# A fused graph-attention and graph-convolution kernel: the four attention units moved together ahead of the convolution, one fold for all, and w2 sums issued sooner

## The chip, the cores and the metric

The kernel runs on one core of a Trainium2 chip (trn2). The metric is the time of one execution in device microseconds; the median of three runs is given. All data is float32. The core has TensorE (PE in the profile, its weight loads PEld), VectorE (DVE), ScalarE (ACT), GpSimd (POOL) and SyncE (SP), whose queue here issues nearly all DMA transfers.

## The reference

There are 16 batches of x, each 1024 nodes by 256 channels, one dense adjacency matrix of 1024 x 1024, and two layers, each followed by a layer norm. The first is attention whose query comes from a graph product; the second is two graph convolutions.

```python
# layer 0, per batch; x: (N=1024, C=256), 4 heads of 64
c_adj = mean over channels of x                      # (N,)
A     = 2 * | |sigmoid(c_j - c_i) - 0.5| - 0.5 |     # (N, N), then made symmetric
g     = relu((x^T @ (adj * A)) * para)               # (C, N)
q     = g^T split in heads;  k, v = x @ kv_w split in heads
att   = softmax(q k^T * scale) v
x     = layernorm(x + att)
# layer 1
h = relu(x @ w1_loop + adj @ (x @ w1_neigh) + b1)    # (N, 128)
h = relu(h @ w2_loop + adj @ (h @ w2_neigh) + b2)    # (N, 256)
x = layernorm(x + (x + h) * 0.5)
```

## The kernel before

**The stages.** The program is one straight list, written out by hand (`tc.manual_schedule()`): each engine runs its instructions in the order in which `run()` (L1196) emits them, and semaphores between engines follow from the tiles that instructions share. There is no planner. An instruction that waits holds up all behind it on its engine; that goes for SyncE's queue of DMA issues too. Tiles of 128 x 1024 come out of a pool of 31 "row" buffers, PSUM tiles out of three "big" ones (128 x 1024) and two "banks" (128 x 512).

In the loop over batches, batch b's attention is computed beside work for three other batches: query, keys and values of batch b+1, the first convolution of batch b−1 (`c1`), the second of batch b−2 (`c2`), and the normalization and output of batch b−3 (`c3`, which exists from b=3 on). Batches 0, 1 and 15 have branches of their own; batches 2 to 14 share one (L1328 to L1372), which the change rewrites. After the loop an epilogue does the convolutions that are left.

**Attention.** A batch has four units: two pairs of heads, times two halves of 512 query nodes. For each unit `scores` (L688 to L715) multiplies keys and queries (L702, two matmuls of 64 rows each per block of 128 keys, eight blocks) and ScalarE takes the exponential (L707, L709). The eight exponentials are added up by VectorE in `collect` (L721, L723); `partial` turns the sum in blocks of 32 x 32 (L728) and reduces it (L731) to a part of the softmax denominator. `outputs` multiplies exponentials and values (L744); `turn` (L750) transposes the result o in blocks of 32. `add` (L757 to L779) sums the parts over partitions with a small matmul against a constant `fold` (L764), takes reciprocals (L770), multiplies o (L774), adds it to the residual in `xB` (L776), and reduces rows for the layer norm (L777). It is called twice in a batch of this branch: for units 0 and 1 inside the convolution (at `turn_to(2)`), for 2 and 3 inside step 1 of the query.

**The query.** The product x^T @ (adj * A) is done with seven block products in place of eight (class `FastQueries`, Strassen's scheme in a form with fewer additions). `left` (L604 to L609) makes sums S of blocks of x on GpSimd. `likeness` (L560, L561) makes the factor A of a row of blocks on ScalarE, `times_adj` (L566) multiplies it with adj on VectorE, and `right` (L619 to L622) makes sums T of weighted blocks. `step(k)` (L647) is then the matmuls for one of four k, seven products of each. Rows 0 and 4 are weighed in `weigh_first`, 1 and 5 in `weigh_second`, 2 and 6, 3 and 7 in `pair`. `KeysValues` makes keys and values in the same way; `kv.sums()` makes its four K sums on VectorE (L423 to L431), and `kv.load()` (L436) fetches weight sums made once at the start.

**The convolution.** `c1.inner()` (L857) multiplies x by w1_neigh. Then `Joined` (L1103) shares the adjacency product of c1's first and c2's second convolution: both need adj times something with 128 columns, and again seven products are made. Its `left` (L1125 to L1128) makes sums R on GpSimd, `product(n)` (L1134) is four matmuls of 512 columns, and `run` (L1137 to L1177) sets the order: products 1, 2, 6, 7, 5, 4, then product 3 in two halves with c2's last products around it. Between products, ScalarE and VectorE move results out of PSUM (L1153, L1156, L1162, L1166, L1169) and form u's halves (L1173 on VectorE, L1174 on GpSimd). `run` takes a table `between`: for each of some places (`turn_to(1)`, `turn_to(2)` and so on) a list of functions that emit other work there. `block_sums` (L953 to L962) forms sums s1 (L958, GpSimd), s2, s4 and s3 (L960 to L962, VectorE) of c2's data, and `last_products` (L979 to L1002) makes seven products with w2's blocks (L971), collecting them by L984 to L1000 and `settle` (L975). A PSUM bank's next product has to wait until the copy or addition before has read it: product 3 of `last_products` goes to the bank that L993 (`u3 + c`) has read. w2's sums and the step of the bias are fetched in `load_sums` (L947 to L950), and `bias` (L1142) copies rows of them to PSUM; the first use is in `run` after `turn_to(2)`.

**Around it.** `c3.statistics()` (L310, L311) takes mean and variance of c3's rows; `deviation` (L315 on VectorE, L316, a power of −0.5, on GpSimd) makes the reciprocal deviation. `finish_aside` (L1020 to L1027) scales the rows on ScalarE and issues the output transfer. `c1.turn_blocks()` transposes c1's result and writes it to DRAM (h1d, L889), from where `load_h1` (L894) takes it at the start of the next batch, with nodes along the partitions. `NodeSums` (L277 to L300) sums x over channels on ScalarE for c_adj.

In batches 2 to 14 before the change, the order on TensorE is: scores of units 0 and 1, their outputs, `inner`, `Joined.run`, scores of units 2 and 3, their outputs, the four steps of the query, keys and values. `channel_major` (the turned x, xT) and the K sums come with the outputs of units 0 and 1.

Of the kernel before, what the change touches and what calls it, by code (L numbers as in the profile page):

```python
# [18 lines left out]
def kernel(  # L19
# [31 lines left out]
    nc = tc.nc  # L51
# [47 lines left out]
    def row_tile(name):  # L99
        return work.tile([P, N], F32, tag="row", name=name, bufs=ROWS)  # L100
# [483 lines left out]
    class FastQueries(Queries):  # L584
# [16 lines left out]
        def block(self, i, j):  # L601
            return self.xb[:, j * TJ:(j + 1) * TJ, ts(i, P)]

        def left(self, eng):  # L604
            s12, s34 = (row_tile(f"S_{self.b}_{k}").rearrange("p (s t c) -> p s t c", s=2, c=P) for k in range(2))
            eng.tensor_add(s12[:, 0], self.block(1, 0), self.block(1, 1))
            eng.tensor_sub(s12[:, 1], s12[:, 0], self.block(0, 0))
            eng.tensor_sub(s34[:, 0], self.block(0, 0), self.block(1, 0))
            eng.tensor_sub(s34[:, 1], self.block(0, 1), s12[:, 1])  # L609
            self.S = [s12[:, 0], s12[:, 1], s34[:, 0], s34[:, 1]]  # L610
# [63 lines left out]
    class Attention:  # L674
# [5 lines left out]

        def __init__(self, b, xB, qT, kT, v):
            self.b, self.xB, self.qT, self.kT, self.v = b, xB, qT, kT, v
            self.parts, self.o, self.pr = {}, {}, {}

            self.rden = small.tile([P, len(UNITS) * FB // S], F32, tag="rden", name=f"rden_{b}", bufs=2)
            self.sums = small.tile([P, NC, NB], F32, tag="sums", name=f"sums_{b}", bufs=2)
# [38 lines left out]
        def partial(self, u):  # L725
            b = self.b
            accB = row_tile(f"accB_{b}_{u}")
            nc.vector.transpose(accB, self.acc)  # L728
            if u % 2 == 0:
                self.part = small.tile([P, 2, N // S], F32, tag="den_part", name=f"den_part_{b}_{u}", bufs=2)  # L730
            nc.vector.tensor_reduce(self.part[:, u % 2, :], by_node(accB), AX.X, ALU.add)  # L731
            self.parts[u] = self.part

        def both_scores(self, pair, summed=True):
            for j in range(NJ):
# [15 lines left out]
        def turn(self, u):  # L751
# [2 lines left out]
            self.o[u] = work.tile([P, FB], F32, tag="o", name=name) if late else row_tile(name)[:, 0:FB]  # L754
            nc.vector.transpose(self.o[u], pav)

        def add(self, *units):  # L757

            b, half = self.b, FB // S
            u0, n = units[0], len(units)  # L760
            pd = bank_psum(f"den_ps_{b}_{u0}")
            den = pd[:, 0:2 * half * n]
            part = [self.parts.pop(u) for u in units][0]
            nc.tensor.matmul(den, fold.rearrange("p a k -> p (a k)"),  # L764
                             part[:, u0 % 2:u0 % 2 + n, :].rearrange("p u k -> p (u k)"), start=True, stop=True)
            den = den.rearrange("p (u s h) -> p u s h", u=n, s=2)
            rden = self.rden[:, u0 * half:(u0 + n) * half].rearrange("p (u h) -> p u h", u=n)
            for s in range(2):
                rows = slice(s * HD, (s + 1) * HD)
                nc.vector.reciprocal(rden[rows], den[rows, :, s, :])  # L770
            for k, u in enumerate(units):
                pair, j = UNITS[u]
                o = by_node(self.o.pop(u))
                nc.vector.tensor_mul(o, o, rden[:, k, :].unsqueeze(2).to_broadcast([P, half, S]))  # L774
                dst = by_node(self.xB[pair][:, ts(j, FB)])
                nc.vector.tensor_add(dst, dst, o)  # L776
                nc.vector.tensor_reduce(self.sums[:, pair, ts(j, half)], dst, AX.X, ALU.add)  # L777
            if u == len(UNITS) - 1:
                join(self.sums)  # L779
# [62 lines left out]
    class GraphConv:  # L842


        def __init__(self, b, xT, nodes=None, x=None):
            self.b, self.xT, self.nodes, self.x = b, xT, nodes, x

        def load_x(self):
            self.x = xpool.tile([P, NT, C], F32, tag="x", name=f"x1_{self.b}")
# [253 lines left out]
    class Joined:  # L1103
# [33 lines left out]
        def run(self, between=None, last=None):  # L1137
# [19 lines left out]
            turn_to(2)  # L1157
            if last:
                bias(third, b2_sb[:, ts(0, P)])
                c2.load_sums()  # L1160
            self.product(6, first, again=True)
            nc.scalar.copy(u1, first)  # L1162
            c1.relu(0, p1)
# [32 lines left out]
    def run():  # L1196
# [58 lines left out]
        for b in range(B):  # L1255
# [18 lines left out]
                q.times_adj(TJ)  # L1274
                q.right(0)

            def two_units(pair, before_first=lambda: None, before_second=lambda: None):
                u = NJ * pair
                att.outputs(u, half_psum, turned=False)
                before_first()  # L1280
                att.turn(u)
                att.outputs(u + 1, turned=False)
                before_second()
                att.turn(u + 1)

            if more and not c1:
                att.both_scores(0)
                NodeSums(q, xb, str(b + 1)).all()
                two_units(0)
                att.both_scores(1)  # L1290
                for t in range(3):
                    q.load(t)
                    q.weigh(t)
                two_units(1)
            elif more and not both:
                att.scores(0)
                att.outputs(0)
                NodeSums(q, xb, str(b + 1)).all()
                kv = KeysValues(b + 1, channel_major(blocked, f"xT_{b + 1}"))
                att.scores(1)  # L1300
                kv.sums()
                att.add(0)
                att.outputs(1)
                for t in (0, TJ):
                    q.load(t)
                c1.inner()
                q.left(nc.gpsimd)
                for t in (0, TJ):
                    q.likeness(t)
                for ij, n in QUARTERS.items():  # L1310
                    store(n, quarters[ij])
                c1.first(quarters, lambda: (att.add(1), adj_sums(quarters, 1), adj_sums(quarters, 2), weigh_first()))
                c1.turn_blocks()
                att.scores(2)
                att.outputs(2)
                for t in (1, TJ + 1):
                    q.load(t)
                    q.likeness(t)
                    q.times_adj(t)
                att.scores(3)  # L1320
                for t in (2, TJ + 2, 3, TJ + 3):
                    q.load(t)
                for t in (2, TJ + 2, 3, TJ + 3):
                    q.likeness(t)
                q.right(1)
                att.add(2)
                att.outputs(3)
            elif more:  # L1328
                att.both_scores(0, summed=False)
                nodes = NodeSums(q, xb, str(b + 1))  # L1330
                att.collect(1, 1, 2, 3)
                nodes.turn()
                att.collect(1, *range(4, NT))
                att.partial(1)
                both.fetch("00", "10")
                c2.load_x()

                def next_xT():
                    ready["xT"] = channel_major(blocked, f"xT_{b + 1}")

                two_units(0, before_second=next_xT)
                if c3:
                    c3.statistics()
                kv = KeysValues(b + 1, ready["xT"])
                kv.sums()
                both.fetch(2, 3)
                nodes.line()
                both.fetch(1)
                nodes.row()
                for t in (0, TJ):  # L1350
                    q.load(t)
                both.fetch(4, "11")
                c1.inner()
                both.left(nc.gpsimd)
                q.left(nc.gpsimd)
                both.run({1: (lambda: q.likeness(0),),
                          2: (lambda: att.add(0, 1), lambda: q.likeness(TJ), lambda: c3 and c3.deviation(), weigh_first)},
                         last=nc.gpsimd)
                c1.turn_blocks()
                att.both_scores(1)  # L1360
                order = (1, TJ + 1, 2, TJ + 2, 3, TJ + 3)
                for t in order:
                    q.load(t)
                for t in order:
                    q.likeness(t)

                def weigh_second():
                    q.times_adj(1)
                    q.times_adj(TJ + 1)
                    q.right(1)  # L1370

                two_units(1, before_second=weigh_second)  # L1372
            else:
                att.both_scores(0)
                two_units(0)
                att.both_scores(1)
                two_units(1, before_second=lambda: att.add(0, 1))
# [38 lines left out]
            elif more:  # L1416
                q.pair(2)
                q.step(0)
                if c3:
                    c3.finish_aside(out[b - 3])  # L1420
                q.step(1, lambda: att.add(*((2, 3) if both else (3,))), 5)
                q.pair(3)
                q.step(2, norm.mean)
                q.load_para()
# [21 lines left out]
            convs[b] = GraphConv(b, norm.x1T, norm.nodes)  # L1446
        c1, c2, c3, c4 = (convs[B - k] for k in (1, 2, 3, 4))
        both = Joined(c1, c2)
        both.fetch("00", "10", 2, 3, 1, 4, "11")
        quarters = fetch_quarters("e", both.far)  # L1450
        c2.load_x()
        c1.inner()
# [79 lines left out]
```

## Time and profile before

| what | value |
|---|---|
| median of 3 runs | 2136.1 us (2135.74 to 2136.44) |
| profiled execution, own time | 2135.35 us |
| its span | 2133.6 us |
| mean granted TensorE clock | 0.997 |
| busy: PE, PEld | 2116.3 us, 1037.2 us |
| busy: DVE, ACT, POOL | 1907.5 us, 1140.1 us, 359.0 us |
| DMA | 346.39 MB, mean 162 GB/s |
| batch 8 by stages (us from the span's start) | scores and outputs of units 0, 1: 1044.85 to 1072.66; convolution: to 1110.53; units 2, 3: to 1138.34; query, keys and values: to 1175.59 |

A page of the profile gives busy times by engine, a row of 40 slices of the span, the DMA queues, the chain of work that ended last, and the costliest groups of instructions. The trace behind it can be asked for a timeline (start and length in us, engine, line, operation, output and inputs, shapes, number of instructions joined, and in brackets how long the engine was idle before it and what released it) and for a table of waits (engine, line and tile that waited, what it waited for, us in total, how many, longest). PE busy includes matmuls that overlap; their ends are modelled, so differences of starts are the better measure.

### The profile page before, as it was taken

The numbers are of one execution on the slowest core, as the hardware profiler recorded it, in microseconds if no ns is written. First come the engines' busy times: TensorE is split into PE (matmuls) and PEld (weight loads), VectorE is DVE, ScalarE is ACT, GpSimd is POOL, SyncE is SP. The second block draws the span as 40 slices with busy tenths as digits, with TensorE's granted clock in tenths as the row PEclk, the third lists the DMA queues.
The fourth block names the chain that finished last, engine by engine and source line by source line (L and its number), as shares of the span: only waits on it lengthen the run. The fifth ranks groups of instructions, "written<-read, shape, count | busy, mean of one in ns | idle before, by whom it ended". The sixth has DMA issues, their size and how long they took to land.

```text
span 2133.6 us, 25172 instructions
## 1 busy us (share of the span) xinstructions
PE 2116.3 (99%) x8734; PEld 1037.2 (49%) x8734; DVE 1907.5 (89%) x2381; ACT 1140.1 (53%) x1669; POOL 359.0 (17%) x209
## 2 busy tenths in 40 slices
PE   9999999999999999999999999999999999999997
PEld 5344444545545455444454444544454444545454
DVE  7899999989999898998989989899898999989874
ACT  5745545556365563655635555454655546556322
POOL 2010120221303113031130301313012130221111
PEclk9999999999999999999999999999999999999998
DMA  9495666637549284592946829377293763925453
GB/s 222 120 170 193 135 221 146 186 107 141 203 125 272 74 165 169 137 262 70 201 141 150 241 69 233 109 163 228 75 259 103 153 212 106 268 87 107 165 192 112
DMA packets 613718, 346.39 MB, mean 162 GB/s; under 512 B 491984, under 2 KB 556880, under 8 KB 613584
## 3 DMA queue, kind: packets, MB, share of 16 engines
q1 hardware_dynamic: 613312, 344.45, 61.2%
q8 instruction: 71, 1.16, 0.2%
q14 instruction: 63, 0.52, 0.1%
q10 hardware_dynamic: 272, 0.26, 0.0%
HBM read 294.45 MB, written 50.20 MB: 162 GB/s over the span
## 4 chain that ended last, share of the span: by engine, by line
PE 98%; DMA 1%; DVE 1%; ACT 0%; POOL 0%; issue 0%; POOLq 0%; SPq 0%; ACTq 0%; DVEq 0%
PE s L702 21%; PE av L744 21%; PE g_ps L647 16%; PE hu_ps L1134 16%; PE v_ps L448 5%; PE k_ps L444 5%; PE hu_ps L971 4%; PE t_ps L857 3%; PE g_ps L574 3%; PE hu_ps L864 2%; PE h_ps L879 1%; PE u_ps L908 1%; DMA out_dram<-x 1%; PE h_ps L971 1%; DMA w_sums<-w_sums 0%; PE den_ps L764 0%
## 5 line engine op out<-in xcount | busy, mean ns | idle before, releaser
L723 DVE TENSOR_TENSOR acc<-acc,pr 128x1024 f32<-128x1024 f32 x384 | 472.2, 1230 | 37.4 <-DVE acc L723 1.4
L702 PE MATMUL s<-qT,kT 64*128 64x512 f32 x2048 | 449.7, 593 | 0.0
L744 PE MATMUL av<-pr,v 128*64 128x512 f32 x2048 | 447.0, 594 | 0.0
L709 ACT ACTIVATE pr<-s 128x1024 f32<-128x1024 f32 x392 | 390.7, 1115 | 75.6 <-PE s L702 75.6
L702 PEld LDWEIGHTS s<-qT,kT 64*128 64x128 f32 x2048 | 196.3, 187 | 232.7 <-issue 183.3
L744 PEld LDWEIGHTS av<-pr,v 128*64 128x64 f32 x2048 | 144.0, 137 | 297.4 <-issue 272.6
L361 POOL TENSOR_TENSOR rstd<-rstd,neg_half 128x32 f32<-128x32 f32 x16 | 99.3, 6203 | 1113.2 <-DVE rstd L359 1113.2
L1134 PE MATMUL hu_ps<-adj,R 128*128 128x512 f32 x480 | 214.3, 594 | 0.0
L560 ACT ACTIVATE wg<-c_row,c_sums 128x1024 f32<-128x1024 f32 x120 | 137.0, 1142 | 81.4 <-DVE den_part L731 60.3
L566 DVE SCALAR_TENSOR_TENSOR wg<-wg,adj 128x1024 f32<-128x1024 f32 x128 | 150.0, 1211 | 3.6 <-ACT wg L561 3.6
L707 ACT ACTIVATE pr<-s 128x512 f32<-128x512 f32 x240 | 142.4, 702 | 0.3 <-PE s L702 0.3
L1134 PEld LDWEIGHTS hu_ps<-adj,R 128*128 128x128 f32 x480 | 89.0, 190 | 100.9 <-issue 99.5
L561 ACT ACTIVATE wg<-wg 128x1024 f32<-128x1024 f32 x128 | 135.3, 1057 | 4.1
L860 ACT COPY t<-t_ps 128x1024 f32<-128x1024 f32 x16 | 16.2, 1012 | 189.6 <-PE t_ps L857 189.6
L647 PE MATMUL g_ps<-wg,S 128*128 128x512 f32 x224 | 115.5, 597 | 0.0
L647 PE MATMUL g_ps<-T,S 128*128 128x512 f32 x224 | 115.5, 597 | 0.0
L647 PE MATMUL g_ps<-wg,x 128*128 128x512 f32 x224 | 109.0, 599 | 0.0
L1134 PE MATMUL hu_ps<-adj,t 128*128 128x512 f32 x240 | 105.7, 592 | 0.0
L1125 POOL TENSOR_TENSOR R<-h 128x512 f32<-128x512 f32 x14 | 28.2, 2012 | 359.5 <-PE av L744 238.8
L721 DVE TENSOR_TENSOR acc<-pr,pr 128x1024 f32<-128x1024 f32 x64 | 77.5, 1211 | 12.3 <-ACT pr L709 12.3
L728 DVE STREAM_TRANSPOSE accB<-acc 128x1024 f32<-128x1024 f32 x64 | 79.7, 1245 | 2.2
L731 DVE TENSOR_REDUCE den_part<-accB 128x32 f32<-128x1024 f32 x64 | 78.1, 1220 | 2.2
(235 smaller groups left out, 3120.1 us busy)
## 6 DMA issues: line engine op xcount, KB each, us to landing
adj<-adjT SPq DMA_DIRECT2D x210, 512.0 KB
adj<-in_adj_dram SPq DMA_DIRECT2D x128, 512.0 KB
para<-in_L_gnn_para_dram SPq DMA_DIRECT2D x32, 512.0 KB
xB_a<-in_x_dram SPq DMA_DIRECT2D x128, 128.0 KB
x1d<-xB_a SPq DMA_DIRECT2D x128, 128.0 KB
x<-x1d SPq DMA_DIRECT2D x16, 1024.0 KB
xB<-in_x_dram SPq DMA_DIRECT2D x120, 128.0 KB
x<-in_x_dram SPq DMA_DIRECT2D x15, 1024.0 KB
```

What stands on the lines that cost most here:

```text
L444: nc.tensor.matmul(dst, self.a[0][n], self.w[n], start=not again, stop=True, skip_group_check=again)
L448: nc.tensor.matmul(dst[:, ts(t, P)], self.w[n][:, ts(t, P)], self.a[1][n], start=not again and t == 0, stop=True, skip_group_check=again o ...
L560: nc.scalar.activation(wg, self.c_row, AF.Abs, bias=self.c_col[:, t:t + 1], scale=-1.0)
L561: nc.scalar.activation(wg, wg, AF.Tanh, scale=-0.5 / C)
L566: nc.vector.scalar_tensor_tensor(wg, wg, 1.0, self.adj.pop(t), op0=ALU.add, op1=ALU.mult)
L647: nc.tensor.matmul(self.p[n], x_n[:, k, :], w_n, start=(k == 0), stop=(k == TJ - 1))
L702: nc.tensor.matmul(halves[s], self.kT[rows, pair, ts(mt, P)], self.qT[rows, pair, ts(j, FB)], start=True, stop=True)
L707: nc.scalar.activation(pr[:, ts(s, FB)], halves[s], AF.Exp)
L709: nc.scalar.activation(pr, ps, AF.Exp)
L723: nc.vector.tensor_add(self.acc, self.acc, prs[mt])
L744: nc.tensor.matmul(pav[s * HD:(s + 1) * HD, :], self.v[:, mt, pair * P + s * HD:pair * P + (s + 1) * HD], prs[mt][:, ts(s, FB)], start=(mt ...
L1134: nc.tensor.matmul(dst, self.x[n][:, k, :], of_rows(rows, k), start=(start and k == 0), stop=(k == TJ - 1), skip_group_check=again)
```

## The change

Four things change. (1) In batches 2 to 14 all four attention units come first, with both of a pair's o tiles in one row (`both_outputs`), and the convolution follows; after it the query's steps come directly. (2) The denominators of all four units stand in one tile, and `add_all` folds them with one matmul of 128 columns, takes reciprocals over all, and multiplies, adds and reduces 1024 columns at a time. It stands at `turn_to(2)` of the convolution, and the two calls of `add` go. (3) Much that stood between the two halves of attention moves: `channel_major` and S come after `inner`, S into the buffers of the blocked x that has been turned (`rows`); S is made before R; K sums and the second `times_adj` move to `turn_to(4)`, behind s1 to s4 on VectorE; the rest of the weighing's likenesses and `finish_aside` move to `turn_to(3)`, that is to the convolution's end, ahead of `turn_blocks`; `weigh_first` moves from `turn_to(2)` to `turn_to(1)`. (4) In the epilogue, `load_sums` is called ahead of `c2.load_x()` and not in `run`.

```diff
-        def left(self, eng):
-            s12, s34 = (row_tile(f"S_{self.b}_{k}").rearrange("p (s t c) -> p s t c", s=2, c=P) for k in range(2))
+        def left(self, eng, rows=None):
+            rows = rows or [row_tile(f"S_{self.b}_{k}") for k in range(2)]
+            s12, s34 = (row.rearrange("p (s t c) -> p s t c", s=2, c=P) for row in rows)
...
+        def both_outputs(self, pair, between=lambda: None):
+            u = NJ * pair
+            row = row_tile(f"o_{self.b}_{pair}")
+
+            def turn(u, j):
+                pav, self.o[u] = self.o[u], row[:, ts(j, FB)]
+                nc.vector.transpose(self.o[u], pav)
+
+            self.outputs(u, turned=False)
+            self.collect(u + 1, 1, 2, 3)
+            between()
+            self.collect(u + 1, 4, 5)
+            turn(u, 0)
+            self.collect(u + 1, 6, 7)
+            self.partial(u + 1)
+            self.outputs(u + 1, half_psum, turned=False)
+            turn(u + 1, 1)
+            self.o[u] = row
+
+        def add_all(self):
+            b, half, n = self.b, FB // S, len(UNITS)
+            pd = bank_psum(f"den_ps_{b}")
+            nc.tensor.matmul(pd[:, 0:n * NB], fold.rearrange("p a k -> p (a k)"),
+                             self.part.rearrange("p u k -> p (u k)"), start=True, stop=True)
+            den = pd[:, 0:n * NB].rearrange("p (u s h) -> p u s h", u=n, s=2)
+            rden = self.rden.rearrange("p (u h) -> p u h", u=n)
+            for s in range(2):
+                rows = slice(s * HD, (s + 1) * HD)
+                nc.vector.reciprocal(rden[rows], den[rows, :, s, :])
+            for pair in range(NC):
+                o = by_node(self.o.pop(NJ * pair))
+                nc.vector.tensor_mul(o, o, self.rden[:, ts(pair, NB)].unsqueeze(2).to_broadcast([P, NB, S]))
+                dst = by_node(self.xB[pair])
+                nc.vector.tensor_add(dst, dst, o)
+                nc.vector.tensor_reduce(self.sums[:, pair, :], dst, AX.X, ALU.add)
+            join(self.sums)
...
             if last:
                 bias(third, b2_sb[:, ts(0, P)])
-                c2.load_sums()
+                if c2.w2 is None:
+                    c2.load_sums()
...
             elif more:
-                att.both_scores(0, summed=False)
+                att.scores(0, 0)
+                att.scores(1, NT, summed=False)
                 nodes = NodeSums(q, xb, str(b + 1))
-                att.collect(1, 1, 2, 3)
-                nodes.turn()
-                att.collect(1, *range(4, NT))
-                att.partial(1)
+                c2.load_x()
+                att.both_outputs(0, nodes.turn)
+                nodes.line()
+                nodes.row()
+                att.scores(2, 0)
+                att.scores(3, NT, summed=False)
                 both.fetch("00", "10")
-                c2.load_x()
-
-                def next_xT():
-                    ready["xT"] = channel_major(blocked, f"xT_{b + 1}")
-
-                two_units(0, before_second=next_xT)
+                for t in (0, TJ):
+                    q.load(t)
+                    q.likeness(t)
+                both.fetch(2, 3)
+                att.both_outputs(1)
+                c1.inner()
+                xT_next = channel_major(blocked, f"xT_{b + 1}")
+                q.left(nc.gpsimd, blocked)
+                both.left(nc.gpsimd)
                 if c3:
                     c3.statistics()
-                kv = KeysValues(b + 1, ready["xT"])
-                kv.sums()
-                both.fetch(2, 3)
-                nodes.line()
+                kv = KeysValues(b + 1, xT_next)
                 both.fetch(1)
-                nodes.row()
-                for t in (0, TJ):
+                for t in (1, TJ + 1):
                     q.load(t)
                 both.fetch(4, "11")
-                c1.inner()
-                both.left(nc.gpsimd)
-                q.left(nc.gpsimd)
-                both.run({1: (lambda: q.likeness(0),),
-                          2: (lambda: att.add(0, 1), lambda: q.likeness(TJ), lambda: c3 and c3.deviation(), weigh_first)},
+
+                def more_weights():
+                    for t in (2, TJ + 2, 3, TJ + 3):
+                        q.load(t)
+                        q.likeness(t)
+                    if c3:
+                        c3.finish_aside(out[b - 3])
+
+                both.run({1: (lambda: q.likeness(1), lambda: q.likeness(TJ + 1), weigh_first),
+                          2: (att.add_all, lambda: c3 and c3.deviation()),
+                          4: (kv.sums, lambda: q.times_adj(1), lambda: q.times_adj(TJ + 1)),
+                          3: (more_weights, lambda: q.right(1))},
                          last=nc.gpsimd)
                 c1.turn_blocks()
-                att.both_scores(1)
-                order = (1, TJ + 1, 2, TJ + 2, 3, TJ + 3)
-                for t in order:
-                    q.load(t)
-                for t in order:
-                    q.likeness(t)
-
-                def weigh_second():
-                    q.times_adj(1)
-                    q.times_adj(TJ + 1)
-                    q.right(1)
-
-                two_units(1, before_second=weigh_second)
...
                 q.step(0)
-                if c3:
-                    c3.finish_aside(out[b - 3])
-                q.step(1, lambda: att.add(*((2, 3) if both else (3,))), 5)
+                if both:
+                    q.step(1)
+                else:
+                    q.step(1, lambda: att.add(3), 5)
...
-        both.fetch("00", "10", 2, 3, 1, 4, "11")
+        both.fetch("00", "10", 2, 3)
+        c2.load_sums()
+        both.fetch(1, 4, "11")
         quarters = fetch_quarters("e", both.far)
         c2.load_x()
```

More of the change, by code (lines that the diff above doesn't have):

```diff
@@ L682, in __init__ @@
             self.b, self.xB, self.qT, self.kT, self.v = b, xB, qT, kT, v
-            self.parts, self.o, self.pr = {}, {}, {}
+            self.o, self.pr = {}, {}
             self.rden = small.tile([P, len(UNITS) * FB // S], F32, tag="rden", name=f"rden_{b}", bufs=2)
@@ L728, in partial @@
             nc.vector.transpose(accB, self.acc)
[L729 to L732, printed above, removed]
+            if u == 0:
+                self.part = small.tile([P, len(UNITS), N // S], F32, tag="den_part", name=f"den_part_{b}", bufs=1)
+            nc.vector.tensor_reduce(self.part[:, u, :], by_node(accB), AX.X, ALU.add)
         def both_scores(self, pair, summed=True):
@@ L762, in add @@
             den = pd[:, 0:2 * half * n]
-            part = [self.parts.pop(u) for u in units][0]
             nc.tensor.matmul(den, fold.rearrange("p a k -> p (a k)"),
-                             part[:, u0 % 2:u0 % 2 + n, :].rearrange("p u k -> p (u k)"), start=True, stop=True)
+                             self.part[:, u0:u0 + n, :].rearrange("p u k -> p (u k)"), start=True, stop=True)
             den = den.rearrange("p (u s h) -> p u s h", u=n, s=2)
@@ L846, in __init__ @@
             self.b, self.xT, self.nodes, self.x = b, xT, nodes, x
+            self.w2 = None
         def load_x(self):
@@ L1275, in weigh_first, with two_units @@
                 q.right(0)
-            def two_units(pair, before_first=lambda: None, before_second=lambda: None):
+            def two_units(pair, before_second=lambda: None):
                 u = NJ * pair
                 att.outputs(u, half_psum, turned=False)
-                before_first()
                 att.turn(u)
```

## The prediction

> **What bounds the kernel now.** I read the busy times first, then TensorE's waits, then the timelines of one ordinary batch (batch 8, from 1044.85 us) and of the end. The page's head:
>
> ```profile
> span 2133.6 us, 25172 instructions
> PE 2116.3 (99%) x8734; PEld 1037.2 (49%) x8734; DVE 1907.5 (89%) x2381; ACT 1140.1 (53%) x1669; POOL 359.0 (17%) x209
> ```
>
> TensorE has work in 99% of the span, and its waits (total, count, longest, us) are three, none of them inside a batch:
>
> ```profile
> PE hu_ps L971 <- ACT h L984: 6.8, 1, 6.8
> PE idle L1206 <- POOL ident masks.py:199: 1.5, 1, 1.5
> PE good_ps L1475 <- DVE x L1054: 1.0, 1, 1.0
> ```
>
> So what is taken from TensorE's list of instructions is gained whole, and anything that comes late for it is lost whole. The 6.8 us wait lies in the epilogue. Its cause, in the timelines of TensorE, SyncE's queue and ScalarE (start, length, ..., idle before and releaser):
>
> ```profile
> 2087.25 1.06 PE L971 MATMUL h_ps<-w2l_sb,h1T 128*128 128x128 f32 x8
> 2095.13 4.62 PE L971 MATMUL hu_ps<-w_sums,last 128*128 128x128 f32 x24 [6.83 <-ACT h L984]
> ```
>
> ```profile
> 2085.64 0.36 SPq L850 DMA_DIRECT2D x<-x1d  x1
> 2086.09 0.53 SPq L950 DMA_DIRECT2D w_sums<-w_sums  x1
> ```
>
> ```profile
> 2093.49 0.59 ACT L1142 COPY hu_ps<-w_sums 128x512 f32<-128x512 f32 x1 [13.65 <-DMA w_sums<-w_sums]
> ```
>
> The w2 sums are issued at 2086.09, behind a load of x (L850) that waits for a buffer, and land at about 2093.5; ScalarE's bias copy waits for them and TensorE for ScalarE.
>
> In batch 8 the convolution, L857 to L971, takes 1072.66 to 1110.53. Its last products, and what VectorE and GpSimd do in it:
>
> ```profile
> 1084.93 0.33 PE L764 MATMUL den_ps<-den_part,fold 128*128 128x64 f32 x2
> ...
> 1109.54 1.06 PE L971 MATMUL hu_ps<-w2l_sb,last 128*128 128x128 f32 x8
> ```
>
> ```profile
> 1081.50 1.68 DVE L423 TENSOR_TENSOR K<-xT 128x512 f32<-128x512 f32 x1
> ...
> 1089.49 0.69 DVE L774 TENSOR_TENSOR o<-o,rden 128x512 f32<-128x512 f32 x1
> ...
> 1107.75 0.69 DVE L993 TENSOR_TENSOR h<-h,hu_ps 128x512 f32<-128x512 f32 x1 [1.97 <-ACT h L992]
> ```
>
> ```profile
> 1082.71 1.61 POOL L607 TENSOR_TENSOR S<-S,x 128x512 f32<-128x512 f32 x1
> ...
> 1093.84 2.55 POOL L316 TENSOR_TENSOR rstd_g<-rstd_g,neg_half 128x8 f32<-128x8 f32 x1 [6.16 <-DVE rstd_g L315]
> ```
>
> Product 3 (1109.54) may start when L993 has left its bank: 1108.44, a slack of 1.1 us. That slack is what the change works against.
>
> **What the skill says.** "SBUF — State Buffer", § Who interferes with whom: a VectorE instruction with two SBUF inputs contends with a GpSimd instruction that reads SBUF; one with a single SBUF input doesn't. The trace agrees: the four K sums (L423 to L431) take 1.65 to 1.75 us against GpSimd's S sums, where the same shape takes 0.69 alone; BATCH_NORM beside GpSimd stays at 0.39. "TensorE: Matmul & The Clock Gate", § Part 1: after an idle window of some 3.4 us the clock halves. Agreed: the gap begins at 2088.3, from 2091.85 to 2098.67 the granted clock is half, and matmuls took 213 ns instead of 112. "TensorEngine Tiling (Array Packing)", § Key Properties: a change of tiling mode drains TensorE. The starts in the trace show 0.14 to 0.2 us at such places (scores, weighted values and convolution use three modes).
>
> **Part 1, the epilogue.** With the w2 sums issued ahead of the blocked x load, bias comes in time. The same 24 matmuls take 2.81 us start to start in batch 15 (2049.23 to 2052.04). Here they start 7.88 after the previous group instead of 0.90 (7.0), and take 4.46 instead of 2.81, of which I count 1.5 as clock: −8.5 us. The next loads land for products needed later; I see nothing else late.
>
> **Part 2, TensorE's list in batches 2 to 14 (13 batches).** Two folds of 64 columns become one of 128: two cost about 0.22 each (own time 0.11 and the gaps around it), the one about 0.27, so −0.18. Two changes of mode go (convolution to scores, weighted values to the sampled product) and one, weighted values to scores, comes: −0.40 + 0.16. Together −0.42 per batch, −5.4 us in 13; from both ends 4.8 to 6.0. This counts only if TensorE still never waits.
>
> **Part 3, VectorE and GpSimd in the convolution.** Attention has 55.6 us of TensorE (4 x 13.9) in one piece; VectorE's work there (four times seven additions of 1.23, a turn of 1.25, a reduction of 1.22: 44 us, and o's turns) fits as before. Then comes the convolution with the fold of all units, first and second weighing, turned x and K sums all in it. I lay VectorE's queue out from T0, the first sampled matmul (L857), with pitches of before: turn of o until 0.7; two xT turns 3.0; statistics 7.2 (4.21); both times_adj 2.3; four T (right) 2.65; snap (L1156) 0.6; two reciprocals of 64x64, 1.15 (64x16 takes 253 ns and 64x32 352, so I set 550 each); then for each half multiply, add, reduce at 1024 wide (0.73 + 0.73 + 0.60, and 0.53 each for the width) 3.65, so 7.3; join 0.1; L315 0.1. Without contention that ends at 21.3.
> GpSimd now writes S into the blocked rows, so after the xT turns (from 2.0), then R: 2.0 to 7.05 for S beside statistics, free of contention; R's four ops from 7.05 stand against times_adj and the T's, all with two SBUF inputs. The four S sums of before cost the K sums 6.83 − 2.6 = 4.2 us, 1.05 each. I take the same 4.2, though the pow (L316, 2.55 here, 1.64 in the epilogue) yielded to both times_adj and cost them nothing; if the first R yields so, 3.1. So L315 is at 21.3 + 4.2 = 25.5, where it was at 20.9.
> Behind it on GpSimd's queue stand the pow, 25.7 to 27.3 (alone now), uT's lower half (L1174) to 28.7, and s1 (L958) to 30.0. VectorE waits for s1 with L960, and behind that one stand L960 to L962, to 31.9; the K sums, 2.6 at 0.65 each when alone, to 34.5; the second times_adj, 2.3, to 36.8; L986 and L975, 1.3; then L993 from 38.1 to 38.8. Product 3 (the third group of w2 products, TensorE's last but one in this stage) waits for L993 and is due at 1109.54 − 1072.66 = 36.9. Stall: 38.8 − 36.9 = 1.9 us. TensorE's own list follows behind it, so the whole batch moves. Stages ahead hold: product 6 needs R2 by 12.2 (has it at 11.8), product 5 the u1 copy behind the snap by 19.3 (18.2), product s6 the s2 sum by 31.3 (30.7). With a contention c in place of 4.2 the stall is c − 2.3.
> Batch 2 has no c3, so neither statistics nor pow: no stall. 12 x 1.92 = +23.0 us. The stall, 2 us, is too short for the clock to drop, which here took 3.6.
>
> **Part 4, moved at no cost.** Two likeness pairs go to ScalarE at 5.8 to 10.3; it is free there (11.7 of 37.9 us busy). The o turns and 1024-wide adds save instructions off TensorE's path. DMA: the number of transfers stays; the adj sums for the products are fetched under the second pair of units, where the DMA engines' share was 0.44 (1110 to 1138), and are needed after them. Most is moved on SyncE's queue: h1d (four), para (two) and kv sums now stand behind the output's transfer, and this waits for ScalarE, which has eight likeness halves (8 x 1.1) and eight scalings (8 x 0.45) from about T0 + 37.5, so until step 0 + 10 (the first sampled product is at T0 + 39.8). Output 1 MB, h1d 0.5, para 1, kv sums 0.5: 3 + 4 + 3 + 2 us at the 300 to 400 GB/s that wide rows reached, and 130 for h1d's short ones, with some 2 for issuing; kv sums land at step 0 + 24, and are needed at + 28.1 (1138.34 to 1166.43). That is 4 us of cover; beyond it each us is a stall. The T's of the later steps come ahead of TensorE: right(1), pair 2 and pair 3 are done by about T0 + 43, 48 and 55, and steps 1, 2 and 3 begin at 46, 52 and 58.5; late T's would show at L647.
>
> **Sum.** 2133.6 − 8.5 − 5.4 + 23.0 = 2142.7 span. The profiled execution took 2135.35, 1.75 over its span, and the median of the runs is 2136.1, 0.75 over that: +2.5, so 2145.
>
> **Rivals.** (A) No stall, on the other side: GpSimd's R sums yield to VectorE, as the pow yielded to the two times_adj, which took 2.36 us together beside it. The place is T0 + 7 to 14; the price is then GpSimd's, not VectorE's, and R2 still comes near 12.2. Below c = 3.5 the change is no longer slower, below c = 2.3 there is no stall: 2133.6 − 13.9 + 2.5 = 2122. For it: 1.1 us of slack at L993 today, and VectorE busy 33.6 of 37.9 us. Against: the S sums of the same shape did not yield but took turns with the K sums in this very stage, and every addition of the list above stands on one queue ahead of L993. (B) The kv sums land late, behind the output and h1d: it shows as a wait of k_ps (L444), and beside the stall above it costs what the 4 us of cover don't hold; 1 us in each of 12 batches gives 2157. For it: SyncE's queue gets 1.5 MB in front of them that lay elsewhere. Against: the cover. (C) The stall is about 1.2 us, where 12 x 1.16 eats the 13.9: 2136, no change; this is the value if one R sum of four yields as the pow did (3.1, stall 0.8, 2132) or two of my pitches run 0.3 short. From 1.2 us up the change is slower.
> That the w2 sums do not land sooner is a small one: +8.5 on any.
>
> **Numbers.** Stall of about 1.9 (1.5 to 2.6) 0.42, its own range 2138 to 2151; A 0.25; C 0.15; B 0.18. 0.2% (4.3 us) is about what a measurement can tell from no change: 2131.8 to 2140.4 is the same. So faster 0.25 (A), same 0.15 (C), slower 0.60. The range 2121 to 2157 takes in A, C and the likeliest, and leaves out most of B and a little below A.
>
> **What would show it.** Right: TensorE has 12 waits of 1.5 to 2.5 us in L971, product 3, released by VectorE's L1030 (L993 of before); no wait in L971 of the epilogue, and 24 matmuls there in 2.8 us; times_adj in the convolution 2.2 us each, not 1.2; L315 near T0 + 25.5. Wrong if times_adj stays 1.2 and L315 is near T0 + 21 (A), or if the wait stands at kv or g (B).

## The result: 4% slower, and the profile after

The changed kernel takes 2220.67 us (median of 4 runs, 2216.1 to 2222.91) against 2135.92 for the kernel before on the same occasions; the ratio is 1.0393 (95% interval 1.0378 to 1.0409). The prediction was 2145 with a range of 2121 to 2157: the sign is right, the size is not. The page's head after:

```profile
span 2221.1 us, 24933 instructions
PE 2135.8 (96%) x8708; PEld 1039.0 (47%) x8708; DVE 1869.2 (84%) x2277; ACT 1131.9 (51%) x1669; POOL 348.2 (16%) x209
```

VectorE has 38 us less to do than before, and TensorE waits. The largest rows of the table of TensorE's waits, and one of VectorE's (us in total, how many, longest):

```profile
PE hu_ps L1008 <- DVE h L1030: 26.0, 12, 2.4
PE av L744 <- ACT pr L708: 21.7, 26, 0.9
PE hu_ps L1171 <- POOL R L1163: 15.2, 13, 3.3
PE hu_ps L1171 <- ACT snap L1200: 4.6, 10, 0.5
DVE acc L722 <- PE av L744: 60.2, 13, 5.4
```

The first row is the forecast stall, at the place named: 12 waits, of 2.43 us in ten batches and 0.81 in two. The 6.8 us of the epilogue is gone. The other rows were not forecast. By stages, an ordinary batch (times between first matmuls, us):

| stage | before, batch 8 | after, batch 7 |
|---|---|---|
| scores and weighted values, four units | 55.6 | 57.5 |
| convolution | 37.9 | 42.7 |
| query, keys, values | 37.2 | 36.9 |
| batch | 130.74 | 137.03 |

13 batches at + 6.3 are 82 us. Five of the 13 are longer by a further 1.7 to 2.2 us (mostly the clock, below), and with smaller pieces the 13 come to + 91.2. The end of the program is 7.6 shorter, its start was 3.9 longer in this execution (not in the variants below): 87.5, the difference of the spans.

**Attention.** TensorE, ScalarE and VectorE in batch 7 (start, length, ..., idle before and releaser):

```profile
965.55 1.88 PE L703 MATMUL s<-qT,kT 64*128 64x512 f32 x8
968.27 13.96 PE L744 MATMUL av<-pr,v 128*64 128x512 f32 x64 [0.84 <-ACT pr L708]
997.00 13.95 PE L744 MATMUL av<-pr,v 128*64 128x512 f32 x64 [0.84 <-ACT pr L708]
```

```profile
967.43 1.28 ACT L708 ACTIVATE pr<-s 128x512 f32<-128x512 f32 x2
```

```profile
1001.63 1.23 DVE L722 TENSOR_TENSOR acc<-pr,pr 128x1024 f32<-128x1024 f32 x1 [4.59 <-PE av L744]
...
1013.69 0.71 DVE L763 STREAM_TRANSPOSE o<-av 128x512 f32<-128x512 f32 x1
```

`both_outputs` gives the first weighted values of a pair to a PSUM bank and the second ones to a big tile; `two_units` had it the other way. The exponentials of key block 6 (L708) still read the banks just then, so TensorE waits 0.84 us, twice a batch. And unit 3's first addition waits 4.59 us on VectorE. It waits for weighted values, which it doesn't read: they release the row buffer that it writes. VectorE's turn of the last o ends at T0 + 3.5 in place of T0 + 0.7 (T0 = 1010.89, the first matmul of `inner`).

**The convolution.** VectorE, GpSimd and TensorE, same batch:

```profile
1020.79 3.42 DVE L566 SCALAR_TENSOR_TENSOR wg<-wg,adj 128x1024 f32<-128x1024 f32 x2
...
1039.24 0.16 DVE L315 TENSOR_SCALAR rstd_g<-mv 128x8 f32<-128x8 f32 x1
...
1051.81 0.68 DVE L1030 TENSOR_TENSOR h<-h,hu_ps 128x512 f32<-128x512 f32 x1
```

```profile
1023.20 2.13 POOL L1163 TENSOR_TENSOR R<-R,t 128x512 f32<-128x512 f32 x1
```

```profile
1025.39 12.26 PE L1171 MATMUL hu_ps<-adj,R 128*128 128x512 f32 x24 [1.85 <-POOL R L1163]
...
1052.55 1.16 PE L1008 MATMUL hu_ps<-w2l_sb,last 128*128 128x128 f32 x8 [0.81 <-DVE h L1030]
```

VectorE starts 2.7 us late, so the turned x, and with it S and R on GpSimd, are late too. R2 ends at T0 + 14.4 where I had 11.8, and product 6 stalls. L315 is at T0 + 28.4, where I had 25.5, and product 3 of the w2 products waits for L1030.

Batches 7 and 8 differ from most of the others. Here the first times_adj gets ahead of R1 (1.21 us, and 2.33 for R1); in batch 6 R1 gets ahead of it (1.28, and 2.34 for the times_adj), and R2 ends at T0 + 13.4. So product 6 waits 1.85 us here and 0.8 there. The longer wait brings 3.4 us at half clock, 1026.49 to 1029.90, which is why the 24 matmuls behind it take 12.26 us instead of 10.5. Two lines of batch 6, with T0 = 873.78, where TensorE also waits 0.46 us for the u1 copy (L1200):

```profile
887.21 7.13 PE L1171 MATMUL hu_ps<-adj,R 128*128 128x512 f32 x16 [0.78 <-POOL R L1163]
...
915.52 1.16 PE L1008 MATMUL hu_ps<-w2l_sb,last 128*128 128x128 f32 x8 [2.43 <-DVE h L1030]
```

What TensorE lost earlier in batch 7, it waits the less at product 3 (0.81 instead of 2.43). The convolution takes 42.7 us in both batches, since L1030 ends at T0 + 41.6 or 41.7 in both: VectorE's queue sets its end.

**The clock.** The granted clock by windows around the end of batch 4's convolution (length, PE busy, PEld, DVE, ACT, POOL, then PEclk, DMA share, GB/s):

```profile
637.20:640.78 3.58, 1.16 (x9) 1.17 (x10) 3.51 (x6) 3.52 (x4) 0.00 (x0) 1.00 0.00 0
640.78:644.20 3.42, 3.42 (x5) 1.38 (x5) 3.35 (x7) 3.39 (x4) 0.00 (x0) 0.50 0.00 0
```

A wait of 2.43 us for L1030 was enough for 3.4 us at half clock, which costs 1.7 us. There are seven such half-clock stretches in the loop (one of them 6.8 us long). Those of batches 7 and 8 cost nothing, because TensorE would have waited at product 3 anyway.

The stretches of one execution all start on a grid of 3.41 us. Laid over the loops of the changed kernel and of the variants `acc_row`, `av_half`, `both` and `r_first` below, the grid has 29 spans at full clock in which TensorE was busy 1.41 us or less, and half clock followed all 29. It followed two of the seven with 1.43 to 1.56 us, and none with more. Two stalls of 2.01 us in `both`, the first inside one span and the second across two (same columns):

```profile
1149.41:1152.82 3.41, 1.40 (x13) 1.21 (x12) 3.34 (x5) 3.29 (x4) 0.00 (x0) 1.00 0.00 0
1152.82:1156.23 3.41, 3.41 (x10) 2.04 (x9) 2.88 (x7) 3.35 (x4) 0.00 (x0) 0.50 0.00 0
...
1282.52:1285.94 3.42, 2.10 (x11) 1.24 (x9) 3.38 (x5) 2.25 (x4) 0.00 (x0) 1.00 0.00 0
1285.94:1289.35 3.41, 2.71 (x12) 1.76 (x13) 3.34 (x8) 3.38 (x4) 0.00 (x0) 1.00 0.00 0
1289.35:1292.76 3.41, 3.41 (x9) 1.52 (x8) 3.34 (x5) 3.35 (x4) 0.00 (x0) 1.00 0.00 0
```

So in these traces it depends on where a stall falls whether it costs 1.7 us more, and the number of stretches in a version is in part chance. Each version has a trace of one execution only.

### The profile page after: what moved, and what is told of

Its sections match the earlier page's. It is cut to its first block, busy times and chain, and to the rows that moved or that the text cites. A ratio compares the mean times of both kernels' runs of the same rounds, so it can differ in the third digit from the quotient of the medians.

```text
span 2221.1 us, 24933 instructions
## 1 busy us (share of the span) xinstructions
PE 2135.8 (96%) x8708; PEld 1039.0 (47%) x8708; DVE 1869.2 (84%) x2277; ACT 1131.9 (51%) x1669; POOL 348.2 (16%) x209
## 4 chain that ended last, share of the span: by engine, by line
PE 53%; DVE 16%; issue 11%; ACT 8%; POOL 7%; DMA 4%; DVEq 0%; SPq 0%; POOLq 0%; ACTq 0%
PE g_ps L648 15%; PE av L744 13%; DVE acc L724 9%; ACT pr L710 5%; PE s L703 5%; PE hu_ps L1171 4%; PE v_ps L448 4%; PE k_ps L444 4%; DMA adj<-adjT 4%; PE g_ps L574 2%; ACT pr L708 2%; PE hu_ps L1008 1%; DVE acc L722 1%; DVE wg L566 1%; POOL R L1163 1%
## 5 line engine op out<-in xcount | busy, mean ns | idle before, releaser
L744 PE MATMUL av<-pr,v 128*64 128x512 f32 x2048 | 447.0, 594 | 21.7 <-ACT pr L708 21.7
L1171 PE MATMUL hu_ps<-adj,R 128*128 128x512 f32 x480 | 223.8, 611 | 19.8 <-POOL R L1163 15.2
L566 DVE SCALAR_TENSOR_TENSOR wg<-wg,adj 128x1024 f32<-128x1024 f32 x128 | 175.8, 1412 | 3.6 <-ACT wg L561 3.6
L708 ACT ACTIVATE pr<-s 128x512 f32<-128x512 f32 x240 | 142.3, 701 | 0.3 <-PE s L703 0.3
L607 POOL TENSOR_TENSOR xB<-x 128x512 f32<-128x512 f32 x13 | 16.5, 1272 | 793.4 <-DVE xT L238 731.4
L648 PE MATMUL g_ps<-wg,xB 128*128 128x512 f32 x208 | 107.9, 600 | 0.0
L648 PE MATMUL g_ps<-T,xB 128*128 128x512 f32 x208 | 106.2, 592 | 0.0
L657 ACT COPY P<-g_ps 128x512 f32<-128x512 f32 x14 | 8.2, 586 | 167.9 <-PE g_ps L648 167.9
```

The lines of the kernel that those rows point to most:

```text
L566: nc.vector.scalar_tensor_tensor(wg, wg, 1.0, self.adj.pop(t), op0=ALU.add, op1=ALU.mult)
L648: nc.tensor.matmul(self.p[n], x_n[:, k, :], w_n, start=(k == 0), stop=(k == TJ - 1))
L708: nc.scalar.activation(pr[:, ts(s, FB)], halves[s], AF.Exp)
L744: nc.tensor.matmul(pav[s * HD:(s + 1) * HD, :], self.v[:, mt, pair * P + s * HD:pair * P + (s + 1) * HD], prs[mt][:, ts(s, FB)], start=(mt ...
L1171: nc.tensor.matmul(dst, self.x[n][:, k, :], of_rows(rows, k), start=(start and k == 0), stop=(k == TJ - 1), skip_group_check=again)
```

## The experiments

Theory 1 was: two things that I had not seen, the bank of the weighted values and the row of unit 3's addition, come on top of a forecast that is right otherwise. Its main rival: VectorE's and ScalarE's queues are full, and what is taken away at one place comes back at another.

### The two unforeseen waits, one by one and together

`av_half`, in `both_outputs`:

```diff
-            self.outputs(u, turned=False)
+            self.outputs(u, half_psum, turned=False)
             self.collect(u + 1, 1, 2, 3)
```

> The changed kernel with one edit: the first weighted values of each pair of units go to a half of a big PSUM tile, as before the change, and not to a bank. Theory 1 (a bank is still being read by the exponential of block 6 when the weighted values start): the 26 waits of L744 for L708, 0.84 us each and 21.7 us in all, go, and nothing takes their place; about 2199 us (2195 to 2203). Rival (attention is bound by ScalarE's exponentials, and the wait comes back later in the stage): 2212 to 2221.

`acc_row`, with the same order of VectorE's instructions:

```diff
                 att.scores(3, NT, summed=False)
+                att.collect(3, 1)
                 both.fetch("00", "10")
...
-            self.collect(u + 1, 1, 2, 3)
+            self.collect(u + 1, *((2, 3) if pair else (1, 2, 3)))
```

> The changed kernel with one edit: the first addition of unit 3 is emitted ahead of the fetches and loads for the convolution, so that its row buffer is taken ahead of them; each engine's order of instructions stays. Theory 1 (VectorE starts the convolution late because that addition waits 4.6 us for a row): the wait goes, statistics start at T0 + 3.0 and not + 5.7, product 6 waits less than 0.3 us, product 3 of the w2 products about 1.9; the convolution takes 39.5 to 40.5 us and not 42.7, and fewer half-clock windows follow; about 2175 us (2165 to 2187). Rival (the convolution is late by its own queues alone, whatever row the addition has): 2210 to 2221.

`both` has both edits.

> Both edits together. Theory 1: what is left is the forecast, a stall of about 1.9 us a batch at product 3 behind the K sums and the second weighing, so 2145 to 2158 us. Rival (one of the two waits hides behind the other): the gain is the larger one's alone, 2170 or more.

| version | us (lowest to highest) | ratio to before, 95% |
|---|---|---|
| av_half | 2203.4 (2203.16 to 2204.07) | 1.0317 (1.03 to 1.0335) |
| acc_row | 2188.7 (2186.93 to 2190.64) | 1.0252 (1.0235 to 1.0269) |
| both | 2156.6 (2155.45 to 2157.69) | 1.0097 (1.008 to 1.0114) |

`av_half`: the 26 waits are gone, and nothing stands in their place in attention (55.6 us again, 57.5 in batch 2 alone). The gain is 17.3 and not 21.7, outside the stated range by 0.4: the loop has 11 half-clock stretches of 3.4 us instead of 8 (long ones counted twice), some 5 us back.
`acc_row`: the row was the cause. That wait on VectorE is gone, no wait for R is left, the convolution takes 40.0 to 40.6 us, and L1030 stalls 24.6 us in 12. In the profiled executions an ordinary batch is 2.65 us shorter (12 of them, 32 us) and batch 2, which had waited longest for R, 6.4. In return, all eight half-clock stretches now lengthen their batches, where in the changed kernel those of batches 7 and 8 did not and two more fell in batch 2: some 7 us back. The time is 1.7 above the range since I had expected fewer of them.
`both`: inside its range, and 64.1 us faster than the changed kernel. VectorE's queue and TensorE in batch 9 of it (T0 = 1247.59):

```profile
1254.81 4.55 DVE L566 SCALAR_TENSOR_TENSOR wg<-wg,adj 128x1024 f32<-128x1024 f32 x2
...
1273.35 0.17 DVE L315 TENSOR_SCALAR rstd_g<-mv 128x8 f32<-128x8 f32 x1
...
1285.91 0.68 DVE L1030 TENSOR_TENSOR h<-h,hu_ps 128x512 f32<-128x512 f32 x1
```

```profile
1286.64 1.16 PE L1008 MATMUL hu_ps<-w2l_sb,last 128*128 128x128 f32 x8 [2.01 <-DVE h L1030]
```

That is the queue of the prediction: times_adj at T0 + 7.2 (forecast 7.2), L315 at 25.8 (25.5), L1030 from 38.3 (38.1), a stall of 2.01 (1.9).

### Is the late R a cost of its own?

`r_first` is the changed kernel with R made ahead of S, so that product 6 has its input in time.

```diff
-                q.left(nc.gpsimd, blocked)
-                both.left(nc.gpsimd)
+                both.left(nc.gpsimd)
+                q.left(nc.gpsimd, blocked)
```

> The changed kernel with one edit: GpSimd makes R ahead of S. Theory 1 (VectorE's late start and its queue set the convolution's end; the late R2 costs nothing by itself): the wait of product 6 for R goes and product 3 waits the more, the convolution stays at 42.7 us or within 0.5 of it; 2212 to 2222 us. Rival (the late R2 is a cost of its own): the convolution is 38.9 to 40.6 us, 2180 to 2197.

Measured: 2199.86 us (2198.54 to 2201.21). TensorE in batch 8 of it:

```profile
1155.23 3.70 PE L1171 MATMUL hu_ps<-adj,R 128*128 128x512 f32 x8 [0.73 <-ACT snap L1200]
...
1175.94 1.16 PE L1008 MATMUL hu_ps<-w2l_sb,last 128*128 128x128 f32 x8 [2.44 <-DVE h L1030]
```

The wait for R is gone, and the convolution still takes 41.95 us instead of 42.7. Of GpSimd's sums, fewer now meet VectorE's (the first times_adj takes 1.63 us instead of 2.34), and L1030 ends at T0 + 40.9 instead of 41.7. Product 3's wait is 2.44 us, as in most batches of the changed kernel (2.43); theory 1 had it grow, and the convolution stay within 0.5 us of 42.7, and neither came out. VectorE's queue still sets the end. In an ordinary batch the late R therefore cost little by itself, as batches 7 and 8 showed already: 1.1 us more of that wait and a half-clock stretch left the convolution as long as it was.

But the time is 12 us under the range, and there the rival has a part. In the profiled executions the loop is 19 us shorter: 9 from 12 ordinary batches, 5.8 from batch 2, where R had been 3.3 us late and the clock had halved behind it, and 4 from fewer half-clock stretches elsewhere (two are left). The start is 3.2 us shorter. Neither theory had the clock in it.

### What makes up the forecast stall

`both_late` and `ksums_late` are `both` with work moved behind L1030: K sums and second times_adj, or the K sums alone.

```diff
-                          4: (kv.sums, lambda: q.times_adj(1), lambda: q.times_adj(TJ + 1)),
-                          3: (more_weights, lambda: q.right(1))},
+                          3: (more_weights, lambda: q.times_adj(1), lambda: q.times_adj(TJ + 1), lambda: q.right(1), kv.sums)},
```

> Both edits, and the K sums and the second times_adj moved from turn_to(4) to turn_to(3), behind L1030 on VectorE. Theory 1: product 3 no longer waits, and the fold, the tiling modes and the epilogue give their 13.9 us: 2120 to 2128 us. Rival (VectorE has no room left, so the 4.9 us come late elsewhere, at the first or second step of the query, L648): 2140 to 2160, with waits of L648 for T or for a bank.

```diff
-                          4: (kv.sums, lambda: q.times_adj(1), lambda: q.times_adj(TJ + 1)),
-                          3: (more_weights, lambda: q.right(1))},
+                          4: (lambda: q.times_adj(1), lambda: q.times_adj(TJ + 1)),
+                          3: (more_weights, lambda: q.right(1), kv.sums)},
```

> The version with both edits (first weighted values in a big tile, unit 3's row early) and with the K sums alone moved behind the second right at turn_to(3); the second times_adj stays ahead of L1030. Theory 1: the stall of 2.05 us at product 3 is shorter than the 2.6 us of the K sums, so it goes, and the T's for step 1 are in time as well: batch 130.3 us, 2121 to 2124 us. Rival (the K sums are late for the keys, or the T's still late at L648 as with both moved): 2126 to 2130.

`both_late` takes 2128.4 us (2127.77 to 2130.19), ratio 0.9966 (0.9955 to 0.9978), 0.4 over theory 1's range. Product 3 waits no more, but a small wait has come at the place that the rival named, for the T's of step 1:

```profile
PE g_ps L648 <- DVE T L622: 2.2, 12, 0.2
```

The query's steps take 24.71 us with it, against 24.26 in `both`. `ksums_late` keeps the T's early and has no such wait; all of its waits over 0.5 us:

```profile
PE s L703 <- DVE o L763: 1.6, 1, 1.6
PE idle L1244 <- POOL ident masks.py:199: 1.5, 1, 1.5
PE good_ps L1512 <- DVE x L1091: 1.0, 1, 1.0
PE s L703 <- ACT qT L581: 0.7, 1, 0.7
```

It takes 2123.65 us (2122.46 to 2126.08), ratio 0.9943 (0.9929 to 0.9957): faster than both kernels. An ordinary batch takes 130.31 us, and no stretch of the loop is at half clock. Steps of 24.26 instead of 24.59 and a convolution of 37.76 instead of 37.87 are 0.44 us less, where Part 2 had 0.42 for the fold and the modes.

`no_S` is `both` with GpSimd's four S sums left out: blocks of x stand in for them, so the query is another one, and the time is that of the same products without these sums.

```diff
-            eng.tensor_add(s12[:, 0], self.block(1, 0), self.block(1, 1))
-            eng.tensor_sub(s12[:, 1], s12[:, 0], self.block(0, 0))
-            eng.tensor_sub(s34[:, 0], self.block(0, 0), self.block(1, 0))
-            eng.tensor_sub(s34[:, 1], self.block(0, 1), s12[:, 1])
-            self.S = [s12[:, 0], s12[:, 1], s34[:, 0], s34[:, 1]]
+            self.S = [self.block(1, 0), self.block(1, 1), self.block(0, 0), self.block(0, 1)]
```

> The version with both edits, with GpSimd's four S sums left out (blocks of x stand in for them), so that R is made beside the statistics. Theory 1 (the 4 us by which times_adj and the T's are stretched are GpSimd's sums, 1.05 us each): times_adj take 1.2 us each, L315 comes near T0 + 21.5, the stall at product 3 goes; 2121 to 2127 us. Rival (VectorE's queue is too long without any contention): the stall stays over 1 us and the time over 2140.

Measured: 2123.38 us (2122.64 to 2124.21), with no wait for L1030 (L1028 in this version). VectorE in batch 8 of it, T0 = 1099.81:

```profile
1107.03 3.60 DVE L566 SCALAR_TENSOR_TENSOR wg<-wg,adj 128x1024 f32<-128x1024 f32 x2
1110.55 0.68 DVE L618 TENSOR_TENSOR T<-wg 128x512 f32<-128x512 f32 x1
...
1122.54 0.17 DVE L315 TENSOR_SCALAR rstd_g<-mv 128x8 f32<-128x8 f32 x1
```

The T's are back at their own lengths, and L315 comes at T0 + 22.7 instead of 25.8. One of R's sums still meets the times_adj (3.60 for the two, not 2.3), so the expected 1.2 each and T0 + 21.5 were too low. Of the 3.0 us by which L315 is earlier, 0.7 is a wait of the first T for TensorE (L620 in `both`) that is gone too; the rest is contention. That is enough to take the stall of 2.0 us away whole: the same queue, without most of the contention, fits.

### The epilogue alone

`tail` is the kernel before with the epilogue's part of the change and nothing else.

```diff
-        both.fetch("00", "10", 2, 3, 1, 4, "11")
+        both.fetch("00", "10", 2, 3)
+        c2.load_sums()
+        both.fetch(1, 4, "11")
...
-                c2.load_sums()
+                if c2.w2 is None:
+                    c2.load_sums()
```

> The kernel before with the epilogue's edit alone (w2 sums fetched ahead of the blocked load of x). As forecast: the 6.8 us wait and the half clock behind it go, 8.5 us; 2127.6 us (2127 to 2128.5). Rival (the loads behind it then come late for a later product): 2130 to 2136, with a new wait of L1134 or of x in the epilogue.

Measured: 2126.66 us (2126.61 to 2127.63), ratio 0.9957 (0.9944 to 0.9971). The 24 matmuls go through without a break, and no other load is late:

```profile
2088.41 2.98 PE L972 MATMUL hu_ps<-w_sums,last 128*128 128x128 f32 x24
2091.23 1.88 PE L1135 MATMUL hu_ps<-adj,R 128*128 128x512 f32 x4
```

So 9.2 us of the gain of `ksums_late` come from one moved DMA, and the whole rebuilding of the batch adds 3.0 us (medians of the same occasion; the two intervals overlap).

## Why the prediction was wrong, point by point

**Right.** Part 1: the epilogue gave 9.2 us alone (8.5). Part 2: 0.44 us a batch (0.42), seen wherever TensorE's wait is gone. Part 3's queue: with a prompt start of VectorE every time in it came within 0.7 us (`both`), and times_adj took 2.3 us each, the sign named for it. The contention is the forecast 4.2 us: in batch 6 of the changed kernel times_adj (2.34 and 2.29 us) and the first two T's (1.75 and 1.64) are 4.25 us over their own lengths of 1.2 and 0.69. In `both` it is 3.5 us, and the first T waits 0.68 us for TensorE (L620) besides, which the prediction didn't have: together L315 is 25.8 − 21.3 = 4.5 us late. Part 4: kv sums and the later T's were in time.

**The step that failed** is one sentence of Part 3: "VectorE's work there ... fits as before". It was an argument from busy time, 44 us in 55.6, and it looked at no waits. Two waits sit in just that stage, 4.6 us of VectorE for a row and 1.7 us of TensorE for a bank; neither is a question of load. I had worked out the T0 of VectorE's queue as if its last work of attention were done by then. What the runs showed in its place: taking the row's wait away gives 32 us alone, the bank's 17, both together 64 us. The batches add up (2.65 and 1.8 us alone, 4.5 together); what is over the sum of 49 is mostly the clock, as `av_half` has three half-clock stretches more than the changed kernel and `both` four fewer.

**The second** is "The stall, 2 us, is too short for the clock to drop, which here took 3.6". In the trace of before there was one gap, and I read a bound off it. The idle window that the prediction cites is more than it takes here, and the measurement decides: stalls of 2.0 us do it where they fall inside one span of the grid (four of 12 in `both`), and those four stretches are 6.8 of the 11.6 us that `both` is above the forecast of 2145.

**Batch 2.** "Batch 2 has no c3, so neither statistics nor pow: no stall" holds for product 3: there are 12 such waits in 13 batches, and in `both` batch 2's convolution takes 37.8 us. But with VectorE late and no statistics to run beside, S as well as R meets times_adj and the T's. R is 3.3 us late there in the changed kernel, and with 6.8 us at half clock the batch is the longest, 139.2 us.

**A sum.** "Its own range 2138 to 2151" lacks the 2.5 us added everywhere else: stalls of 1.5 to 2.6 us give 2140 to 2153. The whole range isn't touched by it.

**The rivals.** Neither A (times_adj would have stayed at 1.2 us) nor B (no wait of k_ps stands in the table) happened. C is not met in the result either; of the runs, `no_S` is what A would have given (2122 forecast, 2123.4 measured), and it takes S away to get there.

## What to carry to other kernels

When stages are put together, redo the question of buffers, not only that of busy time: for each tile written in the new order, ask who read its buffer last, and in a pool that is nearly full, ask in which order the program takes buffers. A fetch that is emitted early can take the buffer of a sum that is needed soon, though no instruction changes its place. Then lay out the queue that ends last and move off it what nobody needs yet: the K sums were wanted some 30 us later and stood in front of TensorE's next input. And price a short stall with the clock in mind: here one of 2 us cost up to 1.7 us more, by where it fell.

## What the runs showed of the hardware that I had not expected

TensorE's clock went to half in steps of 3.41 us (or twice that), most of them after waits of 1.85 to 2.4 us, each step costing 1.7 us where no later wait took it up. How many there are doesn't follow the sum of the waits: `av_half` waits some 19 us less than the changed kernel and has 11 steps in the loop instead of 8; `r_first` has 2 with 64 us of waits in the loop, where the changed kernel has 71. It follows TensorE's busy time within single spans of the grid shown above; no run shifted a stall against the grid on purpose. The Trainium skill, "TensorE: Matmul & The Clock Gate", § Part 1, speaks of an idle window of about 3.4 us that is free-running; the grid of 3.41 us agrees with that, but a span in which TensorE worked 1.41 us was idle enough here, and the measurement decides.
